# An infinity row by column points, image 0 prepared in one piece, and VectorE's operations in another order

## The chip, the cores and the metric

The kernel runs on one core of a Trainium2 chip. The metric is the device time of one execution in microseconds (us). TensorE is called PE, VectorE DVE, ScalarE ACT, GpSimd POOL and SyncE SP, as in the profile. Everything is computed in float32.

## The reference, cut

The input x has 4 images of 256 channels and 64 x 64 pixels. Each output pixel is a weighted sum of 49 neighbours of the same image, the weights coming from a softmax over a convolution; then the result is whitened over groups of 64 channels with the statistics of all images.

```python
k = conv(x, w1, padding=6, dilation=2) + b1        # 256 -> 128 channels, 7 x 7 taps
k = conv(k, w2) + b2                               # 128 -> 49, 1 x 1
attn = softmax(k, axis=1)
shifts = stack([xp[:, :, 2*u:2*u+64, 2*v:2*v+64] for u in range(7) for v in range(7)], axis=1)
y = einsum('bkchw,bkhw->bchw', shifts, attn)       # xp: x padded by 6 on each side
# whitening: mean and 64 x 64 covariance of each channel group, 5 Newton steps
# for its inverse square root, that matrix times the centred y, gain and shift
```

## The kernel before

**The convolution.** w2 is multiplied into w1, which leaves one convolution from 256 channels to 49 logits with 7 x 7 taps at distance 2. Since the distance is 2, even and odd rows and even and odd columns are separate problems. An image lies in two slots in on-chip memory, one for each row parity; the two column parities stay side by side. The 7-tap convolution is computed by evaluation and interpolation at seven points, 0, 1, -1, 2, -2, 1/2 and infinity (number 6, `INF`), first along rows and then along columns:

- `row_weights` and `weights` evaluate the weights at a row point and a column point. This is done once for each pair, at the first image that needs it. Later images load the result from DRAM (`gd`). For row points 4 and 5 the row-evaluated weights wait in DRAM (`kept`) until then.
- `row_eval` evaluates an image at one row point on VectorE and leaves it in one of three buffers `rb`.
- `col_eval` evaluates that at the column points. There is one buffer `xh` for each column point, so the next row's points can be written only when PE has read the present ones.
- `conv_bank` is PE's part: the points of a row are taken in three banks, (1, 2, 0), (3, 4, infinity) and (5). For each, matmuls of 128 columns (line L502) accumulate in one of two PSUM buffers `cv`, and ACT copies the result to `pv` (L512), which has two buffers.
- `col_interp` interpolates a row's seven column points, 22 VectorE instructions of 162 or 144 elements, and writes one plane of `zz`. One of the four output phases needs no arithmetic and is copied by ACT (L567). `row_interp` does the same over the planes, with 576 and 512 elements, and gives the logits. It has two parts: part 0 can start before the last row is there. All arithmetic of these functions goes through `add` (L300), `sub` (L303) and `madd` (L307), which therefore are VectorE's lines in the profile.

Some row points are computed without column points: `direct` convolves the rows as they are with 28 wide matmuls (L608) and needs hardly any VectorE work. Image 0 does this for row points 0, 4, 5 and infinity, and all other images for infinity alone, through `direct_inf`, which loads its weights into a buffer `wi` and leaves its result in a plane of its own, `zi`. So `rows` lists row points 1, 2, 3 for image 0, and 0 to 5 (`ROWS`) for images 1, 2, 3.

**The rest.** `softmax` transposes the logits (L797), takes the maximum (L803) and the exponentials on ACT (L811). `move_terms` and `load_band` bring the weights by way of DRAM and a VectorE transpose (L908) into a band matrix. `first_half` and `second_half` ("a half" below) make transposed blocks of x (L926, copied by ACT at L934), multiply them with the band (`weighted_sum`, L955), store y (L974), and `turn_y` (L987, L995) and `moments` (L1008) collect the covariance. At the end comes the whitening.

**The order.** PE's instructions keep the order in which they are written. Image 0 is written out by hand, and VectorE keeps the written order there too (`strict`). From image 1 on, the program is a list of `conv_step`s. Each convolves one bank, prepares the same bank of the next row, and at a row's last bank interpolates. The halves of the image before are put into gaps of this list: every step has a cost (6, 5 and 2 for the three banks, 12 for the direct infinity), and each time an eighth of the image's cost has passed, a half or a softmax follows. A scheduler orders VectorE, ACT and POOL there by priority, except at an image's end, where `in_order()` fixes VectorE's order. Before, the direct infinity stands ahead of row 0 in images 2 and 3, and after row 0 in image 1.

Of the kernel before, what the change touches and what calls it, by code (L numbers as in the profile page):

```python
# [27 lines left out]
ROWS = (0, 1, 2, 3, 4, 5)  # L28
# [3 lines left out]
def kernel(  # L32
# [222 lines left out]
    zz = apool.tile([P, NP - 1, Q9, W], F32, name="zz")  # L255
    zi = [apool.tile([P, Q9, W], F32, name=f"zi{k}") for k in range(2)]
    for k in range(2):
        nc.gpsimd.memset(zi[k], 0.0)
    ct = apool.tile([P, Q8 * 4 * Q8, 4], F32, name="ct")
    it = ct.rearrange("p a b -> p (a b)")[:, :PT].rearrange("p (q b) -> p q b", q=Q9)  # L260
# [10 lines left out]
    gd = [dram.tile([P, nsl, NSK], F32, name=f"gd{b}") for b in range(NP - 1)]  # L271
# [42 lines left out]

    def keep_weights(br):
        f = (gb5 if br == 5 else gbr).rearrange("p v a r k -> p (v a r k)")
        nc.scalar.mul(f, f, SCALE[br])
        nc.sync.dma_start(kept[br], f)

    def row_weights(br):  # L320
# [8 lines left out]
        if br == 1:  # L329
            add(E, T[6], T[4])  # L330
            add(O, T[5], T[3])
            add(S0, E, O)
            add(E1, T[2], T[0])
# [4 lines left out]
        elif br == 3:  # L338
            madd(E, T[4], 4.0, T[6])
            madd(O, T[3], 4.0, T[5])  # L340
            madd(S0, O, 2.0, E)
            madd(E1, T[0], 4.0, T[2])
            madd(S1, T[1], 2.0, E1)
        elif br == 4:
            madd(S0, O, -2.0, E)
            madd(S1, T[1], -2.0, E1)
        else:
            madd(S0, T[6], 2.0, T[5])
            madd(S0, S0, 2.0, T[4])
            madd(S0, S0, 2.0, T[3])  # L350
            madd(S1, T[2], 4.0, T[0])
            madd(S1, T[1], 2.0, S1)
            add(S1, S1, S1)

    def weights(b, br, i):
# [9 lines left out]
        wt = apool.tile([P, ns, NSK], F32, tag=f"wr{i}", name=f"wr_{b}_{br}_{i}")  # L365
# [7 lines left out]
        elif br in kept:  # L373

            f = rb[0].rearrange("p q r c w -> p (q r c w)")[:, : KS * NSK]
            if i == 0:
                nc.sync.dma_start(f, kept[br])
            f = f.rearrange("p (v a r k) -> p v a r k", v=KS, a=NCC, r=2)
            g = [f[:, v] for v in range(KS)]
        else:  # L380
            g = [gbr[:, v] for v in range(KS)]
        g = [t.rearrange("p a r k -> p (a r k)") for t in g]
        e, o, e1 = (
            ct.rearrange("p a b -> p (a b)")[:, k * NSK : (k + 1) * NSK] for k in range(3)
        )
# [4 lines left out]
        if i == 0:  # L390
            add(e, g0[0], g0[2])
            add(o, g0[1], g0[3])
            add(o0[1], e, o)
            sub(o0[2], e, o)
            add(e1, g1[0], g1[2])
# [4 lines left out]
        elif i == 1:  # L400
            madd(e, g0[2], 4.0, g0[0])
            madd(o, g0[3], 4.0, g0[1])
            madd(o0[3], o, 2.0, e)
            madd(o0[4], o, -2.0, e)
            madd(e1, g1[2], 4.0, g1[0])
# [3 lines left out]
        else:  # L409
            madd(o0[5], g0[0], 2.0, g0[1])  # L410
            madd(o0[5], o0[5], 2.0, g0[2])
            madd(o0[5], o0[5], 2.0, g0[3])
            madd(o1[5], g1[0], 4.0, g1[2])
            madd(o1[5], g1[1], 2.0, o1[5])
# [8 lines left out]
    def row_eval(b, br, rb=rb):  # L423

        for pr in range(2):
# [5 lines left out]
            elif br == 0:  # L431
                nc.scalar.copy(r[2], xs[:, 0])
            for cc in range(NCC):
                X = [xs[:, a, :, cc] for a in range(4)]
                q = [t[:, :, cc] for t in r]
                if br == 3:
                    madd(q[1], X[2], 4.0, X[0])
                    madd(q[2], X[3], 4.0, X[1])
                elif br == 5:
                    madd(q[2], X[0], 2.0, X[1])  # L440
                    madd(q[2], q[2], 2.0, X[2])
                    madd(q[2], q[2], 2.0, X[3])
# [9 lines left out]
        return rb[{1: 2, 2: 0, 3: 0, 4: 1, 5: 2, 0: 2}[br]]  # L452

    def col_eval(src, i):
# [9 lines left out]
        if i == 0:  # L464
            add(EO, X[:, :, 0:2], X[:, :, 2:4])
            add(o[1], E, O)
            sub(o[2], E, O)
            nc.scalar.copy(o[0], X4[0])
        elif i == 1:
            madd(EO, X[:, :, 2:4], 4.0, X[:, :, 0:2])  # L470
            madd(o[3], O, 2.0, E)
            madd(o[4], O, -2.0, E)
            nc.scalar.copy(o[INF], X4[3])
        else:
            madd(o[5], X4[0], 2.0, X4[1])
            madd(o[5], o[5], 2.0, X4[2])
            madd(o[5], o[5], 2.0, X4[3])

    ncv = [0]
    pvs = {}  # L480

    def conv_bank(b, br, i, w):

        if i == 0:
            pvs[b, br] = apool.tile(
                [P, NP, Q9, 2 * Q9], F32, tag="pv", name=f"pv_{b}_{br}", bufs=2
            )
# [23 lines left out]
        with tc.high_priority():  # L511
            nc.scalar.copy(  # L512
                pvs[b, br][:K2, i0 : i0 + len(pts)].rearrange("p n q b -> p (n q b)"),
                cv[:K2, : len(pts)].rearrange("p n q b two -> p (n q b two)"),
            )

    def interpolate(pt, tmp, outs, cut, part=None):

# [8 lines left out]
        if part != 1:  # L527
# [4 lines left out]
            add(s3, c0, c6)  # L532
            sub(s3, tmp, s3)
            madd(s1, tmp, -2.0, s1)
            madd(tmp, tmp, -30.5, s1)
            madd(tmp, s3, 22.5, tmp)
            madd(s1, c0, 1.5, s1)
            madd(s1, c6, -30.0, s1)
            madd(s3, s1, -1.0 / 6, s3)
            sub(s4, s4, s2)  # L540
            madd(tmp, s2, -16.0, tmp)
            add(tmp, tmp, s4)
            madd(outs[0], lo(s1), 1.0 / 6, hi(c0))
            add(outs[2], lo(c6), hi(s3))
        if part != 0:
            madd(hh, tmp, -1.0 / 9, hh)
# [5 lines left out]
    def phases(t):  # L552

        return [t[:, :, bass.ds(4 + a - R if a < R else 0, Q8, 4)] for a in range(4)]

    def col_interp(b, br, part=None):
        pv = pvs[b, br]
        pt = {c: pv[:K2, i] for i, c in enumerate(ORDER)}
        outs = phases(zz[:K2, br].rearrange("p q (w two) -> p q w two", two=2))
        cut = lambda t, k: t[:, :, 2 * k : 2 * (k + Q8)].rearrange("p q (b two) -> p q b two", two=2)  # L560
        t = it
        if part is not None:

            t = pvs[b, ROWS[-2]][:, 0]
        interpolate(pt, t[:K2], outs, cut, part)
# [818 lines left out]
```

## Time and profile before

| what | value |
|---|---|
| median of 3 runs | 761.5 us (761.24 to 763.82) |
| profiled execution | 767.08 us, span 765.3 us |
| granted PE clock | 0.978 |
| PE busy | 710.7 us (93%) |
| DVE busy | 630.3 us (82%), 1312 instructions |
| ACT busy | 332.4 us (43%) |
| POOL busy | 34.4 us (4%) |
| image 0 ends (last interpolation of rows) | 171.3 us |
| image 1 ends | 315.1 us |
| image 2 ends | 462.6 us |
| image 3 ends | 600 us |

The span runs from the first to the last instruction of the profiled execution, and that execution was 5.6 us longer than the median of the runs. A group line of the profile gives the source line, engine and operation, the tiles (out<-in), shape and count, then busy time and the mean of one instruction in ns, then the idle time of the engine ahead of them and what ended most of it. [...]

### The profile page before, as it was taken

The page shows a single profiled execution, that of the slowest core. Times are in us where ns is not written, and L with a number is a line of the kernel's source. Part 1 is how long each engine was busy: PE and PEld are TensorE (multiplying, and loading weights), DVE is VectorE, ACT ScalarE, POOL GpSimd, SP SyncE. Part 2 cuts the span into 40 slices and gives each one's busy share as a digit, 9 for nine tenths or more (in the row PEclk, how much of TensorE's full clock was granted, in tenths as well). Part 3 has the DMA queues.
Part 4 walks back from the last instruction along what each step waited for, and adds up shares of the span by engine and source line. Part 5 has one row for each costly group of instructions (what it writes and reads, how often), then busy time and mean ns, then how long its engine had stood idle before and what let it go on. Part 6 is the DMA issues. An engine that isn't in the chain of part 4 may idle for free.

```text
span 765.3 us, 18542 instructions
## 1 busy us (share of the span) xinstructions
PE 710.7 (93%) x7512; PEld 538.0 (70%) x7512; DVE 630.3 (82%) x1312; ACT 332.4 (43%) x958; POOL 34.4 (4%) x48
## 2 busy tenths in 40 slices
PE   6989899969899999989999999999999889998996
PEld 1449564365798887779988967798898768885322
DVE  3769999999899999989996899699979775645565
ACT  2413241025555454366444443635435473322464
POOL 0410000020000010001000100000000000000000
PEclk9999999979999999999999999999999999999999
DMA  8991110042654393056734920533532233362487
GB/s 323 238 322 65 39 75 38 1 155 68 200 153 156 122 351 91 20 160 205 235 120 141 313 70 1 155 90 110 166 88 80 49 115 128 115 251 111 190 362 327
DMA packets 59773, 114.76 MB, mean 150 GB/s; under 512 B 22903, under 2 KB 42024, under 8 KB 58920
## 3 DMA queue, kind: packets, MB, share of 16 engines
q1 hardware_dynamic: 55992, 94.71, 37.5%
q0 software_dynamic: 3696, 18.88, 7.2%
q8 instruction: 59, 0.97, 0.5%
q14 instruction: 26, 0.21, 0.1%
HBM read 66.23 MB, written 47.33 MB: 148 GB/s over the span
## 4 chain that ended last, share of the span: by engine, by line
DVE 43%; PE 32%; ACT 5%; issue 5%; DMA 2%; SPq 0%; DVEq 0%; ACTq 0%
PE y L955 10%; PE cv L502 7%; DVE xh L307 5%; PE tp L1324 4%; DVE rb L307 3%; DVE pv L307 3%; DVE zz L307 3%; DVE ct L307 3%; DVE ct L300 3%; DVE band L908 3%; PE sig L1008 3%; PE tp L987 2%; PE tp L926 2%; DVE pv L303 2%; DVE rb L300 2%
## 5 line engine op out<-in xcount | busy, mean ns | idle before, releaser
L502 PE MATMUL cv<-xh,wr 128*49 128x128 f32 x4368 | 253.7, 278 | 14.3 <-DVE xh L300 11.5
L502 PEld LDWEIGHTS cv<-xh,wr 128*49 128x49 f32 x4368 | 247.3, 125 | 19.9 <-issue 12.9
L955 PE MATMUL y<-band,xb 128*128 128x224 f32 (+2 forms) x640 | 153.4, 379 | 12.5 <-ACT xb L934 8.3
L955 PEld LDWEIGHTS y<-band,xb 128*128 128x128 f32 x640 | 111.2, 196 | 34.4 <-ACT xb L934 10.8
L974 ACT ACTIVATE slot<-y,pivot 128x512 f32<-128x512 f32 x53 | 36.7, 740 | 60.0 <-PE y L955 60.0
L512 ACT COPY pv<-cv 113x486 f32<-113x486 f32 (+1 forms) x63 | 29.8, 474 | 74.9 <-PE cv L502 73.7
L995 ACT COPY yt<-tp 128x256 f32<-128x256 f32 x128 | 45.5, 379 | 34.8 <-PE tp L987 33.8
L926 PE MATMUL tp<-ident,slot 128*128 128x128 f32 x256 | 50.3, 299 | 7.1 <-ACT yt L995 7.1
L987 PE MATMUL tp<-ident,slot 128*128 128x128 f32 x256 | 52.0, 299 | 4.0 <-ACT xb L934 1.4
L908 DVE STREAM_TRANSPOSE band<-band 128x960 f32<-128x960 f32 (+1 forms) x48 | 50.8, 1059 | 4.9 <-DMA band<-sd 4.8
L987 PEld LDWEIGHTS tp<-ident,slot 128*128 128x128 f32 x256 | 41.3, 205 | 13.9 <-issue 4.5
L926 PEld LDWEIGHTS tp<-ident,slot 128*128 128x128 f32 x256 | 40.0, 206 | 14.4 <-ACT yt L995 9.0
L857 ACT COPY zt<-d 32x112 f32<-32x112 f32 (+2 forms) x156 | 45.0, 288 | 1.7
L811 ACT ACTIVATE d<-tp,mx 128x49 f32<-128x49 f32 x128 | 37.0, 336 | 15.1 <-DVE mx L806 15.1
L307 DVE SCALAR_TENSOR_TENSOR xh<-ct 128x512 f32<-128x512 f32 x42 | 27.7, 681 | 12.2 <-PE cv L502 12.0
L934 ACT COPY xb<-tp 128x256 f32<-128x256 f32 x87 | 30.4, 376 | 15.8 <-PE tp L926 15.2
L1008 PE MATMUL sig<-yt 128*64 128x65 f32 x1024 | 36.9, 225 | 0.0
L1008 PEld LDWEIGHTS sig<-yt 128*64 128x64 f32 x1024 | 32.5, 138 | 6.0 <-issue 4.4
L608 PE MATMUL cv<-slot,wi 128*49 128x496 f32 (+3 forms) x168 | 34.8, 571 | 0.0
L934 DVE COPY xb<-tp 128x256 f32<-128x256 f32 x41 | 16.4, 421 | 22.2 <-PE tp L926 22.2
L307 DVE SCALAR_TENSOR_TENSOR pv<-pv 113x162 f32<-113x162 f32 x105 | 33.5, 319 | 1.0
L419 ACT ACTIVATE wr<-wr 128x392 f32<-128x392 f32 (+1 forms) x36 | 17.3, 512 | 31.1 <-DVE wr L300 18.8
(224 smaller groups left out, 999.9 us busy)
## 6 DMA issues: line engine op xcount, KB each, us to landing
out_dram<-out SPq DMA_DIRECT2D x32, 512.0 KB, 3.4
sd<-zt SPq DMA_DIRECT2D x16, 896.0 KB, 3.9
slot<-in_x_dram POOLq DMA_DIRECT2D x12, 1024.0 KB, 9.6
band<-sd SPq DMA_DIRECT2D x128, 84.0 KB, 2.1
wr<-gd SPq DMA_DIRECT2D x15, 588.0 KB, 3.8
wr<-gd SPq DMA_DIRECT2D x15, 490.0 KB, 3.6
spill<-slot POOLq DMA_DIRECT2D x3, 2048.0 KB, 8.4
back<-spill SPq DMA_DIRECT2D x3, 2048.0 KB, 7.7
```

The lines of the kernel that those rows point to most:

```text
L300: return in_turn(TT(o, a, b, ALU.add))
L307: return in_turn(STT(o, a, f, b, ALU.mult, ALU.add))
L502: nc.tensor.matmul(cv[h * HB : h * HB + KT, k, sr : sr + n, sc : sc + n], wv[:, sc, sr, cc], xh[bc][:, :n, h * NCC + cc, :n], start=(j == ...
L811: nc.scalar.activation(d[:, h, i], lt[i // NI][:, i % NI, h, :KT], AF.Exp, bias=mx[:, i, h : h + 1], accum_out=s[:, h, i : i + 1],)
L857: ins = nc.scalar.copy(o, i)
L908: nc.vector.transpose(f, f)
L926: nc.tensor.transpose(t[:, cc * P : (cc + 1) * P], xt[:, cc, CR * m : CR * (m + 1), bass.ds(pc, SW, 2)], ident,)
L934: (nc.vector.tensor_copy if tail else nc.scalar.copy)(xb, t[:, :C])
L955: nc.tensor.matmul(ps[:, cc, q0 - half * HALF : q1 - half * HALF, :], xb[:, cc * P : (cc + 1) * P], rhs, start=(k == 0), stop=(k == len(PI ...
L987: nc.tensor.transpose(t[:, cc * P : (cc + 1) * P], yt[:, cc, CR * i : CR * (i + 1), bass.ds(pc, SW, 2)], ident,)
L995: nc.scalar.copy(yb.rearrange("p a g c -> p (a g) c")[:, :, :GW], t[:, :C].rearrange("p (e c) -> p e c", c=GW),)
L1008: nc.tensor.matmul(sig[g * GW : (g + 1) * GW, cc], yb[:, cc, g, :GW], yb[:, cc, g], start=(count[0] == 0 and cc == 0), stop=(count[0] == 4 ...
```

## The change

It has four parts.

1. **Infinity in images 2 and 3.** `ROWS` begins with `INF`, so that images 2 and 3 compute this row by column points like the others: half a row of matmuls, since only one of its two taps exists. Its weights are evaluated in image 2 and kept in DRAM. `direct_inf` and its buffer are gone. Image 1 still uses `direct` for it, but the call stands at the end of image 0's part and accumulates in another PSUM buffer.
2. **Image 0.** All row points are evaluated, convolved or brought to `direct` first, and all interpolation follows. Weights and column points are interleaved (`both0`). Row 0 of image 1 is prepared partly before and partly after the last interpolation. The first softmax comes at the start of image 1.
3. **Neighbours on VectorE.** In `row_weights`, `weights`, `row_eval`, `col_eval` and `interpolate` the same operations stand in another order, so that an instruction rarely needs the result of the one just before it. For this `pv` is one tile with three slots instead of two buffers, and ACT's copy L567 of most rows is put behind the next row's second eviction (`later`). `row_interp` uses `ct` for its temporary; `zi` is gone.
4. **Costs.** The planner's costs follow, so gap 0 of images 2 and 3 now falls after the first bank of row 0 and gap 1 after the first bank of row 1.

```diff
-ROWS = (0, 1, 2, 3, 4, 5)
+ROWS = (INF, 0, 1, 2, 3, 4, 5)
...
+    NV = 3
+    pv = apool.tile([P, NV, NP, Q9, 2 * Q9], F32, name="pv")
...
+    kept[INF] = dram.tile([P, KS * NSK // 2], F32, name="gi")
+    nc.sync.dma_start(kept[INF], tap[:, UPOS[3]].rearrange("p v a k -> p (v a k)"))
...
         if i == 0:
             add(e, g0[0], g0[2])
             add(o, g0[1], g0[3])
+            add(e1, g1[0], g1[2])
             add(o0[1], e, o)
             sub(o0[2], e, o)
-            add(e1, g1[0], g1[2])
...
+            elif br == INF:
+                nc.scalar.copy(r[1], xs[:, 3])
...
+    def both0(src, br, i):
+
+        g = col_ops(src, i)
+        next(g)
+        nxt.update(weights(0, br, i, lambda: next(g)))
+        for _ in g:
+            pass
...
+        if i == 1:
+
+            while later:
+                tc.add_manual_dep(
+                    later.pop()().ins,
+                    last.ins.name,
...
             add(s3, c0, c6)
+            madd(s1, tmp, -2.0, s1)
             sub(s3, tmp, s3)
-            madd(s1, tmp, -2.0, s1)
             madd(tmp, tmp, -30.5, s1)
+            sub(s4, s4, s2)
             madd(tmp, s3, 22.5, tmp)
             madd(s1, c0, 1.5, s1)
+            madd(tmp, s2, -16.0, tmp)
             madd(s1, c6, -30.0, s1)
+            if part is None:
+                add(tmp, tmp, s4)
             madd(s3, s1, -1.0 / 6, s3)
-            sub(s4, s4, s2)
-            madd(tmp, s2, -16.0, tmp)
-            add(tmp, tmp, s4)
...
+        if b > 0:
+
+            t = pv[:K2, (at + 2) % NV, NP - 1].rearrange("p q b -> p (q b)")
...
+        if part is None and b > 0 and br != ROWS[-2]:
+            later.append(end)
+        elif part != 0:
+            end()
...
-    rows += [(b, br) for b in range(1, B) for br in ROWS]
+    rows += [(b, br) for b in range(1, B) for br in ROWS[1 if b == 1 else 0 :]]
...
-    nxt.update(weights(0, 3, 0))
-    col_eval(xr, 0)
-    direct0(0, 1)
-    nxt.update(weights(0, 3, 1))
-    col_eval(xr, 1)
-    nxt.update(weights(0, 3, 2))
+    for i in three:
+        both0(xr, 3, i)
+        if i == 0:
+            direct0(0, 1)
+    for i in three:
+        bank(2, i)
     row_weights(4)
     keep_weights(4)
     xrs[4] = row_eval(0, 4)
-    col_interp(0, 1)
-    col_eval(xr, 2)
-    bank(2, 0)
-    bank(2, 1)
     direct0(4, 0)
-    bank(2, 2)
     row_weights(5)
...
+    col_interp(0, 1)
     col_interp(0, 2)
     direct0(4, 1)
+    direct0(5, 0)
     col_interp(0, 3)
     row_interp(0, 0)
-    direct0(5, 0)
-    for i in three:
-        prepare(NR0, i)
+    prepare(NR0, 0)
     direct0(5, 1)
     row_interp(0, 1)
+
+    direct(1, INF, 0, acc[:, 0], [tap[:, UPOS[3], v] for v in range(KS)])
+    prepare(NR0, 1)
+    prepare(NR0, 2)
...
-        inf = (12, lambda b=b: direct_inf(b))
         if b == 1:
-
-            steps[:3] = [
-                *steps[:3], (0, lambda: soft(0, 0)), inf, (0, lambda: soft(0, 1)),
-            ]
-        else:
-            steps.insert(0, inf)
+            steps.insert(0, (0, lambda: soft(0, 0)))
+            steps.insert(4, (0, lambda: soft(0, 1)))
```

## The prediction

> **What bounds the kernel now.** First the engines' busy time and, beside it, the chain that ended last:
>
> ```profile
> PE 710.7 (93%) x7512; PEld 538.0 (70%) x7512; DVE 630.3 (82%) x1312; ACT 332.4 (43%) x958; POOL 34.4 (4%) x48
> ...
> DVE 43%; PE 32%; ACT 5%; issue 5%; DMA 2%; SPq 0%; DVEq 0%; ACTq 0%
> ```
>
> The reader is to see that the busier engine isn't the one that the chain names most: PE and VectorE take turns. So I read VectorE by stage (PE, PEld, DVE, ACT, POOL after the stretch and its length):
>
> ```profile
> 50.00:171.30 121.30, 106.88 (x1050) 69.68 (x1048) 116.50 (x227) 31.43 (x64) 6.73 (x8) 0.95 0.21 77
> 171.30:315.70 144.40, 138.21 (x1634) 112.41 (x1631) 139.26 (x306) 72.50 (x229) 5.78 (x5) 0.99 0.48 154
> 315.70:463.20 147.50, 141.81 (x1840) 124.04 (x1840) 131.13 (x268) 72.78 (x226) 8.03 (x7) 0.99 0.51 162
> 463.20:601.00 137.80, 132.01 (x1764) 120.18 (x1761) 123.75 (x258) 67.92 (x220) 0.15 (x1) 0.99 0.33 98
> ```
>
> These are image 0 and the convolutions of images 1, 2 and 3. VectorE has 4.8 and 5.1 us to spare in the first two, and 16.4 and 14.1 us in the last two. Images 0 and 1 are its own; in 2 and 3 it and PE wait for each other. After 601 us comes the tail, which the change doesn't touch.
>
> What neighbours cost shows in VectorE's timeline (start, duration):
>
> ```profile
> 303.29 0.32 DVE L303 TENSOR_TENSOR pv<-pv 113x162 f32<-113x162 f32 x1
> 303.64 0.33 DVE L300 TENSOR_TENSOR pv<-pv 113x162 f32<-113x162 f32 x1
> 304.00 0.33 DVE L303 TENSOR_TENSOR pv<-pv,pv 113x162 f32<-113x162 f32 x1
> ...
> 337.06 0.32 DVE L307 SCALAR_TENSOR_TENSOR pv<-ct,pv 113x162 f32<-113x162 f32 x1
> 337.30 0.32 DVE L300 TENSOR_TENSOR pv<-pv 113x162 f32<-113x162 f32 x1
> 337.54 0.32 DVE L303 TENSOR_TENSOR pv<-pv 113x162 f32<-113x162 f32 x1
> ```
>
> Same shape, same duration, but starts 0.36 us apart where each needs its predecessor, 0.24 where none does: **0.12 us for a dependent neighbour**. One instruction between is enough. The same difference stands at 512 elements (0.60 against 0.72) and 576 (0.67 against 0.79). So I cost VectorE by starts, not by durations.
>
> Last, PE's timeline at the change to image 2 and the waits of ACT:
>
> ```profile
> 300.81 11.59 PE L608 MATMUL cv<-slot,wi 128*49 128x512 f32 x56
> ...
> 320.19 1.12 PE L797 MATMUL tp<-ident,lgx 113*128 113x113 f32 x8
> 321.24 10.03 PE L502 MATMUL cv<-xh,wr 128*49 128x128 f32 x176
> ...
> 335.25 0.52 PE L926 MATMUL tp<-ident,slot 128*128 128x128 f32 x2 [1.88 <-ACT yt L995]
> ```
> ```profile
> ACT zz L567 <- DVE pv L307: 50.4, 17, 7.1
> ```
>
> L608, the direct infinity row, fills PE while VectorE ends image 1. The half after the first softmax is slow (331.20 to 342.57, 11.4 us, where others take 7.7) because exponentials and copies fill ACT. And 17 times ACT stands in the copy L567 until VectorE has ended an interpolation.
>
> [...]
>
> **The change, part by part.**
>
> *VectorE's order.* In the two built programs' lists, instructions that wait for their immediate predecessor fall from 276 to 118: 158 x 0.12 = **19.0 us** less. By stage: image 0 130 to 48 (-9.8), image 1 30 to 6 (-2.9), image 2 45 to 21 (-2.9), image 3 58 to 30 (-3.4); the tail is as before.
>
> *The infinity row of images 2, 3.* PE: 28 wide matmuls (11.6 us) become 52 of 128 columns, half a row; a row of 208 records took 11.76 us, so 5.9. Saved 5.7 us twice. VectorE gains per image 9 instructions of column points (two of 1024 at 1.14, seven of 512 at 0.60: 6.5 us) and 22 of interpolation (5.2 us), and once 20 of weights (98 columns, 0.17: 3.4 us). That is +15.1 in image 2, +11.7 in image 3. With the order: -9.8, -2.9, **+12.2, +8.3**, in all +7.8 us. ACT gains two copies of 128x1024 (1.05 each) and three evictions (0.5 each) per image, and loses one; it is 43% busy. SP's queue loses the `wi` loads and gains one load of kept weights, three stores and three loads of gd (wr<-gd lands in 3.8 us), issued a row ahead; the load writes rb[0], free by then. Cover gone, each would cost its 4 us once. POOL's memsets after gpool.release wait for the moved L608; it ends earlier than before.
>
> *Image 0 first; image 1's infinity ahead.* VectorE bound from 50 us, so image 0 ends at about 171.3 - 9.8 = 161.5. L608 of image 1 (11.6 us) goes into PE's gaps there and is no longer ahead of row 0.
>
> *Image 1* is VectorE's: row_interp ended at 315.1, now 315.1 - 9.8 - 2.9 = 302.4.
>
> *Change to image 2.* After that VectorE must still do 9.1 us (summed from the list: rest of the infinity row, and of row 0 its first column points) until row 0's bank 0 can start: 311.5. It ends 5.4 us later (316.9); the half, which the planner now puts behind it since the infinity row counts 6.5 and not 12, and the softmax transposes (7.6 + 1.1) end at 325.6. Before, the same work was done at 321.24 + 5.4 = 326.6. **Of 12.7 us, 1 is left**: PE had L608 and the half done while it waited, now it waits with nothing to do. Then row 0's other banks (6.4) to 332; row 1's bank 0 needs points that the list puts at 302.4 + 31.0 = 333.4; it ends at 338.8, the next half and softmax at some 348 if ACT is freer there (+0.5), against 343.62 + 7.2 = 350.8. So **-3**.
>
> *Change to image 3.* Counted from 420.60, where PE starts row 4's last banks. Before: row 0's bank 0 ended at 473.60 + 5.4, 58.4 later, half and softmax within. Now VectorE needs 12.2 us to the start of row_interp (433.47 before, less 0.7 by the order) and 33.3 (list) to row 0's first points: 45.5. PE needs only 11.8 + 5.5 + 6.4 + 9.3 + 5.9 = 38.9, so it idles 6.6. Then 5.4 + 7.6 + 1.1: 59.6. **+1 to +4, taken +3**, as transposes of the band come between.
>
> *Softmax of image 2* (483.56 to 494.71, 11.2): its half now comes a bank later, away from the exponentials: 3.5 less, of which I take **-2**. *L567 deferred, third pv slot:* PE waited 15.2 us for ACT's xb and yt copies between 150 and 603; a fifth of it: **-3**. Alone on a busy VectorE it would be 0, at best -8.
>
> Sum: -3 + 3 - 2 - 3 = -5. The profiled execution took 767.08 us (span 765.3), 5.6 above the median; it becomes 762, and the median 761.5 becomes **756**.
>
> **Rivals.**
> 1. *The early gain is kept whole.* PE's waiting at the image changes is filled (VectorE catches up in its 16.4 us of slack). Then -12.7 stays, +3 falls away, with part of ACT: 748, at best 744. For it: the slack. Against: the lists put row 0's points behind the infinity row. Chance 0.2.
> 2. *PE's chain decides.* From 202 us PE's records follow each other; the 11.4 us saved turn into idle time, and ACT brings nothing: 761. That VectorE's order does not matter[...] ends here or worse. Chance 0.15.
> 3. *Slower.* VectorE's slack in images 2, 3 is waiting at image changes for PE to free the single xh buffers (xh L307 waited 12 us for L502), and can't be filled. Then +12.2 + 8.3 comes in full against -12.7: +8, 769. It decides once less than about 8 of the 30 us of slack is used. For it: the infinity row falls where VectorE has no pause. Against: in the middle of both images PE is the later one. Chance 0.2.
>
> **How the numbers follow.** The forecast has 0.45 (751 to 760). Half a per cent (3.8 us) is about what a measurement here can tell: faster is under 757.7, slower above 765.3. Forecast: 0.38 faster, 0.07 same; rival 1 all faster; rival 2 same; rival 3 slower. Faster 0.58, same 0.22, slower 0.20. The range 744 to 768 reaches from the best of rival 1 to just short of rival 3's own value, and leaves out the upper part of rival 3 alone.
>
> **What would show it.** Right: VectorE x1394; interpolation starts 0.24 apart; image 0 ends near 161, image 1 near 302; PE idle 5 to 8 us before row 0 of image 3, named by DVE xh. Wrong: image 0 not 8 us earlier (the order), or image 2's middle 10 us earlier (rival 1), or row 0 of image 3 later than 474 (rival 3).

## The result and the profile after

The change makes the kernel slower by half a per cent. The median of 20 runs is 765.44 us (761.8 to 776.25), that of the kernel before 761.52 us (756.27 to 764.05, 20 runs). The ratio is 1.0059, 95% interval 1.004 to 1.0078. A second set of runs gave 1.0046 (1.0025 to 1.0068). The prediction had 756 us, a gain.

The page after, engines and chain, as they were shown of before:

```profile
PE 698.6 (92%) x7608; PEld 539.3 (71%) x7608; DVE 643.0 (85%) x1394; ACT 342.8 (45%) x980; POOL 33.7 (4%) x45
...
DVE 44%; PE 41%; ACT 5%; DMA 4%; issue 4%; SPq 1%; DVEq 0%; ACTq 0%
```

PE has 12 us less to do, VectorE 13 us more, and the counts are the forecast ones (7608 and 1394). By stage, in the same stretches as before:

```profile
50.00:171.30 121.30, 119.29 (x1194) 71.32 (x1190) 114.99 (x237) 39.66 (x107) 6.66 (x7) 1.00 0.21 75
171.30:315.70 144.40, 123.12 (x1618) 113.06 (x1619) 139.56 (x328) 70.03 (x200) 5.64 (x4) 0.94 0.49 152
315.70:463.20 147.50, 136.07 (x1819) 124.06 (x1820) 135.23 (x288) 77.33 (x236) 8.03 (x7) 0.98 0.52 165
463.20:601.00 137.80, 132.99 (x1764) 121.97 (x1761) 129.11 (x284) 68.58 (x222) 1.00 (x6) 0.98 0.34 102
```

In the stretch of image 1 PE now stands idle for 21 us. The edges are those of the first trace of before, and the changed kernel's images end elsewhere. Cut at each kernel's own image ends, images 2 and 3 read as follows, first before (its second trace, r4_before, see below), then after:

```profile
309.30:455.60 146.30, 140.37 (x1839) 123.24 (x1839) 131.09 (x267) 72.63 (x226) 8.03 (x7) 1.00 0.51 163
455.60:592.20 136.60, 130.72 (x1767) 119.58 (x1764) 124.20 (x259) 67.97 (x220) 0.15 (x1) 1.00 0.32 99
...
299.40:457.00 157.60, 145.59 (x1962) 132.82 (x1958) 145.14 (x312) 81.32 (x245) 8.03 (x7) 0.99 0.53 165
457.00:596.60 139.60, 131.46 (x1765) 121.30 (x1766) 133.21 (x290) 68.13 (x221) 0.15 (x1) 0.97 0.33 99
```

VectorE has 14.1 and 9.0 us more to do, and the two images took 11.3 and 3.0 us longer. Of the 27.6 us that it had to spare, only 8.8 were taken up: 2.8 in image 2 and 6.0 in image 3.

The new order does what it was meant to do. VectorE's timeline, in the last interpolation of image 1's columns:

```profile
287.54 0.32 DVE L303 TENSOR_TENSOR pv<-pv 113x162 f32<-113x162 f32 x1
287.77 0.32 DVE L310 SCALAR_TENSOR_TENSOR pv<-pv 113x162 f32<-113x162 f32 x1
288.01 0.32 DVE L306 TENSOR_TENSOR pv<-pv 113x162 f32<-113x162 f32 x1
```

Neighbours start 0.24 us apart where before they started 0.36 apart. What it is worth is lost at the image changes. PE's timeline, images 1 to 2 and 2 to 3:

```profile
297.06 2.87 PE L531 MATMUL cv<-xh,wr 128*49 128x128 f32 x48
303.48 4.12 PE L531 MATMUL cv<-xh,wr 128*49 128x128 f32 x40 [3.55 <-DVE xh L310]
308.31 6.42 PE L531 MATMUL cv<-xh,wr 128*49 128x128 f32 x112 [0.71 <-ACT pv L541]
...
322.27 1.17 PE L846 MATMUL tp<-ident,lgx 113*128 113x113 f32 x8
```
```profile
450.66 2.67 PE L531 MATMUL cv<-xh,wr 128*49 128x128 f32 x40 [0.56 <-DVE xh L310]
460.68 8.08 PE L531 MATMUL cv<-xh,wr 128*49 128x128 f32 x112 [7.34 <-issue]
...
476.28 1.12 PE L846 MATMUL tp<-ident,lgx 113*128 113x113 f32 x8
```

The reader is to see the idle times in brackets: between the infinity row's banks PE has nothing to do. "issue" at 460.68 says that the profile shows no releaser, but VectorE's timeline does:

```profile
456.34 0.69 DVE L310 SCALAR_TENSOR_TENSOR lgx<-zz 113x512 f32<-113x512 f32 x1
456.95 0.69 DVE L310 SCALAR_TENSOR_TENSOR xh<-rb 128x512 f32<-128x512 f32 x1
457.55 1.22 DVE L303 TENSOR_TENSOR ct<-rb 128x1024 f32<-128x1024 f32 x1
458.69 0.69 DVE L310 SCALAR_TENSOR_TENSOR xh<-xh,rb 128x512 f32<-128x512 f32 x1
459.29 0.68 DVE L303 TENSOR_TENSOR xh<-ct 128x512 f32<-128x512 f32 x1
459.89 0.68 DVE L310 SCALAR_TENSOR_TENSOR xh<-xh,rb 128x512 f32<-128x512 f32 x1
```

Column point 5 of the infinity row takes three dependent operations. The first comes right after the last operation of image 2's row interpolation, each of the others behind one of row 0's, and the third ends at 460.57, 0.1 us before PE goes on.

Behind this gap of 7.34 us PE is slow as well. The same stretch by windows; the third number from the end is the granted clock:

```profile
453.40:457.40 4.00, 0.00 (x0) 0.00 (x0) 3.90 (x6) 2.05 (x4) 0.00 (x0) 0.99 0.44 125
457.40:464.20 6.80, 3.52 (x34) 3.55 (x36) 6.80 (x12) 0.68 (x2) 0.00 (x0) 0.50 0.07 15
464.20:476.00 11.80, 11.80 (x150) 10.77 (x147) 11.77 (x28) 4.07 (x10) 0.00 (x0) 1.00 0.20 62
```

For the first 3.3 of these 6.8 us PE was still idle, which costs nothing more. The rest slowed the 112 records of matmuls at 460.68: they took 8.08 us, where 112 took 6.42 at full clock (at 308.31). From there PE works without a pause to the softmax at 476.28, so these 1.7 us are lost. At the change to image 2 the half clock (303.8 to 307.2) lay on the 40 records at 303.48, and there it cost nothing, for VectorE had column point 5 of the infinity row ready only at 308.16:

```profile
307.48 0.68 DVE L310 SCALAR_TENSOR_TENSOR xh<-xh,rb 128x512 f32<-128x512 f32 x1
```

**Which trace of before to compare with.** The first one (767.08 us) is longer than every one of the other 20 executions. The waits of VectorE in it, from 30 to 60 us, hold a wait for image 0's input:

```profile
DVE rb L300 <- DMA slot<-in_x_dram: 6.5, 1, 6.5
```

A second trace of the same kernel (r4_before, 756.32 us, span 754.5) has no such wait, and its stages lie 6 to 9 us earlier. It is near the shortest execution of before (755.98), as the changed kernel's trace (761.8) is its shortest, so these two are compared. The changed kernel's other trace (r0_after) lies 1.9 to 3.6 us later at the marks of the table, so a difference of 1 to 2 us between neighbouring marks says little. Marks are the softmaxes' first transposes on PE. With the change a first softmax has row 0's first bank ahead of it (5.4 us), a second has 7.2 us more ahead of it (row 0's third bank, row 1's first); both are taken off.

| mark | before, second trace | changed | difference, like for like | forecast |
|---|---|---|---|---|
| image 1, first softmax | 313.7 | 322.3 | +3.2 | -1 |
| image 1, second | 334.9 | 343.1 | +1.0 | -3 |
| image 2, first | 464.9 | 476.3 | +6.0 | 0 |
| image 2, second | 485.4 | 496.7 | +4.1 | -2 |
| image 3, first | 597.8 | 603.6 | +5.8 | -5 |
| span | 754.5 | 760.0 | +5.5 | -5 |

### The profile page after: what moved, and what is told of

Its sections match the earlier page's. It is cut to its first block, busy times and chain, and to the rows that moved or that the text cites. A ratio compares the mean times of both kernels' runs of the same rounds, so it can differ in the third digit from the quotient of the medians.

```text
span 760.0 us, 18845 instructions
## 1 busy us (share of the span) xinstructions
PE 698.6 (92%) x7608; PEld 539.3 (71%) x7608; DVE 643.0 (85%) x1394; ACT 342.8 (45%) x980; POOL 33.7 (4%) x45
## 4 chain that ended last, share of the span: by engine, by line
DVE 44%; PE 41%; ACT 5%; DMA 4%; issue 4%; SPq 1%; DVEq 0%; ACTq 0%
PE cv L531 9%; PE y L1004 8%; PE acc L668 6%; DVE xh L310 6%; DVE pv L310 5%; DVE rb L310 4%; PE tp L1370 4%; DVE ct L310 3%; DVE band L957 3%; DVE ct L303 3%; DVE zz L310 3%; DVE pv L306 2%; PE tp L1036 2%; PE tp L975 2%; PE sig L1057 2%
## 5 line engine op out<-in xcount | busy, mean ns | idle before, releaser
L531 PE MATMUL cv<-xh,wr 128*49 128x128 f32 (+1 forms) x4576 | 268.8, 279 | 19.5 <-issue 7.3
L531 PEld LDWEIGHTS cv<-xh,wr 128*49 128x49 f32 x4576 | 260.6, 126 | 25.5 <-issue 18.0
L1004 PE MATMUL y<-band,xb 128*128 128x224 f32 (+2 forms) x640 | 151.2, 374 | 15.0 <-ACT xb L983 12.9
L1004 PEld LDWEIGHTS y<-band,xb 128*128 128x128 f32 x640 | 109.6, 193 | 36.4 <-ACT xb L983 16.0
L541 ACT COPY pv<-cv 113x486 f32<-113x486 f32 (+1 forms) x69 | 33.2, 483 | 101.8 <-PE cv L531 101.5
L310 DVE SCALAR_TENSOR_TENSOR pv<-pv 113x162 f32<-113x162 f32 x215 | 63.8, 318 | 0.5
L310 DVE SCALAR_TENSOR_TENSOR xh<-ct 128x512 f32<-128x512 f32 x46 | 30.3, 683 | 10.2 <-PE cv L531 10.2
L983 ACT COPY xb<-tp 128x256 f32<-128x256 f32 x87 | 30.4, 376 | 12.7 <-PE tp L975 12.0
L306 DVE TENSOR_TENSOR pv<-pv 113x162 f32<-113x162 f32 x112 | 34.6, 319 | 0.4
L668 PE MATMUL acc<-slot,tap 128*49 128x496 f32 (+3 forms) x168 | 34.6, 569 | 0.0
```

The lines of the kernel that those rows point to most:

```text
L306: return in_turn(TT(o, a, b, ALU.subtract))
L310: return in_turn(STT(o, a, f, b, ALU.mult, ALU.add))
L531: nc.tensor.matmul(cv[h * HB : h * HB + KT, k, sr : sr + n, sc : sc + n], wv[:, sc, sr, cc], xh[bc][:, :n, h * NCC + cc, :n], start=(j == ...
L668: nc.tensor.matmul(ps[h * HB : h * HB + KT, :, w0:w1_], w[v][:, cc], xs[:, :, cc, w0 + d : w1_ + d], start=(j == 0), stop=(j == len(order) ...
L983: (nc.vector.tensor_copy if tail else nc.scalar.copy)(xb, t[:, :C])
L1004: nc.tensor.matmul(ps[:, cc, q0 - half * HALF : q1 - half * HALF, :], xb[:, cc * P : (cc + 1) * P], rhs, start=(k == 0), stop=(k == len(PI ...
```

## The experiments

All ratios are to the kernel before on the same chip, with 95% intervals. Two theories stood at the start: the waits of PE (W), or the granted clock (C).

**r0_after: the changed kernel again.**

> The changed kernel again, for a second trace of it beside others on one chip. Two theories of why it is 4 us slower than before although its one trace is 5 us shorter. Theory W (waits): the infinity row's VectorE work at the two image changes leaves TensorE idle for 7 + 4 us and takes back what the order and image 0 gave; then this trace again shows gaps of about 3.5 and 7 us ahead of row 0 of images 2 and 3, and the time is 763 to 767. Theory C (clock): the stages are shorter, but the granted TensorE clock is lower in most executions than in that trace (0.970 to 0.976 against 0.978), each 0.001 being some 0.8 us; then the time of single executions follows their clock, and the execution at the highest clock takes about 762.

Measured: 764.55 us, ratio 1.0046. The gaps are there again (4.2 us at 275, 3.3 at 302, 7.4 at 456). Times follow the clock: the 45 executions of before that were measured beside it have a correlation of -0.92 between time and clock, with 0.49 us for 0.001. But before has a median clock of 0.980 and the changed kernel one of 0.975, and a line through each kernel's executions (29 of the changed one, from both sets) gives 761.5 and 761.9 us at 0.980. So most of the difference shows as clock. The traces say where the lower clock comes from: between 50 and 650 us PE runs at half clock for 6.8 us in r4_before (clock 0.991), for 23.9 us in the first trace of before (0.978) and for 27.3 us in both traces of the changed kernel (0.978 and 0.975); in r4_before and the changed kernel each piece stands behind an idle time of 1.6 us or more. In all 18 traces every idle time of PE over 2.4 us in that stretch was followed by half clock within 5 us of its start. In the changed kernel's first trace these were 5.4 us of idle time from 184.5 (half clock from 187.7), 4.3 from 273.3 (276.4), 3.6 from 299.9 (303.8) and 7.3 from 453.3 (457.4). So in these traces half clock follows the gaps, and what theory C saw is, as far as they show, a part of W's price.

**r4_before: the kernel before, a second trace.** Nothing is edited.

> The kernel before, once more, for a second trace. In its first trace (767.08 us) VectorE waited 6.5 us for image 0's input at 46.91; in the traces of the changed kernel and of the two part versions there is no such wait. If that wait was an accident of the one execution, this trace has none, its stages lie about 6 us earlier, and it takes 756 to 763 us; then all gains that the prediction counted against the first trace hold, but 6 us of what the two traces differ by is no gain. If it belongs to the kernel's order, it is here again, and the time is near 767.

Measured: 756.32 us, no wait for the input. The wait was an accident of the first execution.

**r1_order: the new order alone.**

The kernel before, with the changed kernel's `row_weights` and `interpolate`, and the same exchanges in `weights` and `row_eval`, such as:

```diff
-            add(o0[1], e, o)
-            sub(o0[2], e, o)
             add(e1, g1[0], g1[2])
+            add(o0[1], e, o)
+            sub(o0[2], e, o)
```

> The kernel before, with the new order of VectorE's operations in row_weights, weights, row_eval and interpolate alone: dependent neighbours fall from 276 to 172, 12.5 us of VectorE's time. By theory W it keeps a good part, since it adds no row: 752 to 757. By theory C the clock falls[...], and it gains little: 758 to 762 with a clock below that of the kernel before. If VectorE's order doesn't matter at all: 761.5.

Measured: 755.03 us, ratio 0.9938 (0.9917 to 0.9959). The order is a gain by itself, and the clock did not fall with it but rose (median 0.988). Its first softmax of image 1 comes at 311.6, 2.0 us ahead of r4_before, and the later marks 3 us ahead. That is about half of the 6.5 us; the rest goes with the clock: at 0.988 the line through the executions of before gives 757.6.

**r2_direct: the change with the direct infinity row in images 2 and 3.**

```diff
-ROWS = (INF, 0, 1, 2, 3, 4, 5)
+ROWS = (0, 1, 2, 3, 4, 5)
...
+        else:
+            steps.insert(0, (12, lambda b=b: direct_inf(b)))
```

> The changed kernel with the infinity row of images 2 and 3 computed directly as before, ahead of row 0 and at a cost of 12 in the plan (its weights are loaded into rb[1]); image 0, the order, pv's slots and the later copy are those of the change. Theory W: TensorE has its 11.6 us of work at the image changes again, VectorE 26.8 us less: 5 to 8 us faster than the changed kernel, 756 to 760. Theory C: within 3 us of the changed kernel, at a clock as low.

Measured: 757.27 us, ratio 0.9961 (0.9937 to 0.9984). The column-point rows cost 0.85 to 1 per cent, some 7 us; without them the change gains in the median. Its shortest execution (755.67) is hardly shorter than that of before (755.98). From the first softmax of image 1 to that of image 2 this version takes 147.4 us, the changed one 154.0.

**r7_old0: r2_direct with image 0 in the old order.**

Image 0's part is that of the kernel before, and behind it stands image 1's direct infinity (against the kernel before):

```diff
     row_interp(0, 1)
+    direct(1, INF, 0, acc[:, 0], [tap[:, UPOS[3], v] for v in range(KS)])
```

> The version with the direct infinity in images 2 and 3 (757.3 us), with image 0 written out in the order of the kernel before, image 1's direct infinity still at the end of that part. The order alone gave 755.0. If image 0's new order costs those 2 us (it leaves two parts of row 0's preparation to image 1, where VectorE has no time to spare): 754 to 756. If pv's third slot and the later copy cost them: 757 to 759.

Measured: 758.51 us, 0.9968 (0.9952 to 0.9984), the same as r2_direct. Image 0's order neither brings nor costs anything that can be told. What separates both from the order alone (some 2 us, with intervals that overlap) is then among pv's slots, the later copy, the other temporary, image 1's infinity ahead and the place of image 0's softmaxes; it was not taken apart further. It shows as clock: a median of 0.979 and 0.980 here, against 0.988 with the order alone, which at 0.49 us for 0.001 is worth 4 us.

**r3_gap: the half ahead of row 0's first bank.**

```diff
-                        (cost * len(taps(br)) / 2, lambda k=k, i=i: conv_step(k, i))
+                        (cost, lambda k=k, i=i: conv_step(k, i))
```

> The changed kernel with the infinity row's banks counted as 6, 5 and 2 in the plan instead of half: the first half of images 2 and 3 then comes ahead of row 0's first bank, and the second after its second bank, as before the change. Theory W: TensorE does a half (8 us) while VectorE prepares row 0, so the gaps there nearly go: 4 to 8 us faster than the changed kernel, less up to 3 us if the second half falls among the exponentials again. Theory C: the gaps go, but the time follows the clock: within 3 us of the changed kernel.

Measured: 764.52 us, 1.0042 (1.0029 to 1.0056), as the changed kernel. The gaps stayed, 3.4 and 7.4 us, because they lie between the infinity row's own banks, ahead of where the half was put. So this edit didn't put the theories to the test.

**r5_fill: the half right behind the infinity row's first bank.**

```diff
-        for cost, f in steps:
+        for n, (cost, f) in enumerate(steps):
...
-            if at * NPC >= (j + 1) * whole:
+            if n == 0 if b > 1 and j == 0 else at * NPC >= (j + 1) * whole:
```

> The changed kernel with the first half of images 2 and 3 put right behind the infinity row's first bank, where TensorE stood idle for 3.6 and 7.3 us and then ran at half clock for 3.4 and 6.8 us. Theory W (TensorE's waiting is the loss): both gaps are filled and no clock is lost there: 752 to 758. Theory D (VectorE is the bound at the image changes, and TensorE's idle time only shows it): row 0 of image 3 starts no earlier than before this edit, gaps appear behind the half instead, 762 to 766.

Measured: 767.77 us, 1.0088 (1.0055 to 1.012). Both gaps are filled, and the wait stands one row later and is longer:

```profile
334.00 8.27 PE L531 MATMUL cv<-xh,wr 128*49 128x128 f32 x96 [8.35 <-DVE xh L303]
```

This is row 1's first bank in image 2. Theory W falls. D stands in kind, though the time lies above its range: around this wait VectorE is the later one (busy 24.77 of 25 us from 325 to 350), and filling PE's gaps moved its idle time and did not remove it.

**r6_mid: the infinity row between rows 2 and 3.**

```diff
-ROWS = (INF, 0, 1, 2, 3, 4, 5)
+ROWS = (0, 1, 2, INF, 3, 4, 5)
```

> The changed kernel with the infinity row between rows 2 and 3 of images 2 and 3 instead of ahead of row 0: its VectorE work (11.7 us an image) then falls into the middle, where TensorE is the later one, and the image changes have neither it nor a direct convolution. Theory W: TensorE has 5.9 us less to do at the changes, but row 0 is ready 9 us earlier: 755 to 760. Theory D: VectorE is relieved where it is the bound: 752 to 757. If the place doesn't matter and only the sum of VectorE's work does: 763 to 766.

Measured: 762.5 us, 1.0012 (0.9997 to 1.0027). Some 2 us better than ahead of row 0, less than W and D said, and next to what was written for the case that the place doesn't matter: new gaps of 5.0 us at 373 and 3.5 at 518 came up in the middle. So the image change is not the only place where the row costs.

**r8_xh5, r9_xh5d: the last bank prepared ahead of row_interp,** in the changed kernel and in r2_direct.

```diff
                     col_interp(b, br, 1)
+                    if k + 1 < len(rows):
+                        prepare(k + 1, i)
                     row_interp(b, 1)
...
                 col_interp(b, br)
                 if last:
+                    prepare(k + 1, i)
                     row_interp(b, 0)
```

> The changed kernel with the last bank of the next row prepared (the three operations of column point 5, and its weights) between col_interp and row_interp at an image's end, in the fixed order; in the changed kernel two of the three slip in between row_interp's operations and the last comes behind it, and TensorE waits 4.3 us in image 1 (trace at 273 to 287) and 7.3 us ahead of row 0 of image 3. Theory S (the new order starves this chain: row_interp's operations, now independent, always go first): both waits fall to under 2 us and the half clock behind them goes; 757 to 761. Theory D (VectorE is simply the bound there, and the wait moves to the next row, as when the half was moved): 763 to 767.

> The same edit on the version with the direct infinity in images 2 and 3 (757.3 us), where TensorE waits 5.6 us at 281 for column point 5 of image 1's last row and runs at half clock for 6.8 us after it. There VectorE has 26.8 us less to do, so both theories differ less: by S 751 to 755; if the wait moves on, 756 to 758.

Measured: r8 768.69 us, 1.0099 (1.0072 to 1.0127); r9 756.27 us, 0.9933 (0.9909 to 0.9957). In r2_direct PE waited in image 1 for the same three operations, which the scheduler had put between those of row_interp:

```profile
286.98 0.88 PE L531 MATMUL cv<-xh,wr 128*49 128x128 f32 x6 [5.60 <-DVE xh L310]
```

In r9 that wait is gone (a shorter one, 2.8 us for a copy of ACT, stands at 284), and the first softmax of image 1 comes at 313.3 instead of 317.5. Its time is 1 us better, within the intervals, and in the range written for a wait that moves on. In r8 the wait moved: 9.1 us at 299, for the infinity row's points, and the time lies above both ranges. So where the row is direct theory S holds for the wait and not for the time; where it is not, D holds.

**r10_noint: without the infinity row's interpolation.**

```diff
+        if br == INF:
+            for a, c in ((0, 0), (2, 1), (1, 2)):
+                add(outs[a], cut(pt[c], 0), cut(pt[5], 1))
+        else:
...
```

> The changed kernel with 19 of the 22 operations of the infinity row's column interpolation left out in images 2 and 3 (its planes get other values; everything else is computed as before): 4.5 us of VectorE an image less, nothing on TensorE, and no transfer. TensorE never waits for this interpolation directly. By theory D time falls by nearly what VectorE saves, 9 us less what it waits elsewhere: 756 to 760. If TensorE's waits come from the order of single operations and not from VectorE's sum: 762 to 765.

Measured: 762.69 us, 1.002 (1.0006 to 1.0035). Nine us of VectorE bring 2. The 7.4 us gap is untouched. VectorE's sum alone is not what decides.

**r11_rb1: the infinity row's weights by way of rb[1].** In the changed kernel's image 1, ACT's and PE's timelines show:

```profile
276.85 0.27 ACT L405 COPY wr<-rb 128x98 f32<-128x98 f32 x1 [5.10 <-DMA rb<-gi]
277.03 0.27 ACT L406 COPY wr<-rb 128x98 f32<-128x98 f32 x1
277.20 0.36 ACT L983 COPY xb<-tp 128x256 f32<-128x256 f32 x1
```
```profile
277.62 1.17 PE L1004 MATMUL y<-band,xb 128*128 128x96 f32 x4 [4.32 <-ACT xb L983]
```

The load into rb[0] waits for row 5's weights there, ACT waits for the load, xb's copy waits behind it, and PE for xb.

```diff
-            f = rb[0].rearrange("p q r c w -> p (q r c w)")[:, : KS * nk]
+            f = rb[1 if br == INF else 0].rearrange("p q r c w -> p (q r c w)")[:, : KS * nk]
...
-                nc.scalar.copy(r[1], xs[:, 3])
+                nc.scalar.copy(r[0], xs[:, 3])
```

> The changed kernel with the infinity row's kept weights loaded into rb[1] and its image rows copied to rb[0], instead of the other way round. In the changed kernel the load into rb[0] has to wait for row 5's weights there; ACT's copy of the infinity row's weights stands 5.1 us for it (trace at 276.85), the copy of xb queued behind it comes late, and TensorE idles 4.3 us in a half and then runs at half clock for 6.8 us. Theory Q (this queue is a part of the loss): the idle time at 273 goes, image 1 ends 4 to 7 us earlier on TensorE, 758 to 762. If VectorE is the only bound there: 763 to 766.

Measured: 763.85 us, 1.0033 (1.0017 to 1.005). ACT's wait is gone, but PE then waits 4.8 us at 281 for column point 5 and the first softmax of image 1 is no earlier (322.7). The jam is real and hidden behind VectorE.

**r12_warm, r13_warmd: extra work in the gaps,** in the changed kernel and in r9_xh5d.

```diff
+    def warm(n):
+        t = tp()
+        for _ in range(n):
+            pe(nc.tensor.transpose(t[:, :P], ident, ident))
...
         conv_bank(b, br, i, w)
+        if br == INF and i == b - 2:
+            warm(11 if b == 2 else 22)
```

In r13 the condition is `(b, br, i) == (1, 1, 2)`, with `warm(16)`.

> The changed kernel with TensorE kept busy in the two gaps of the infinity rows by extra transposes of the identity whose result nobody reads: 11 (3.2 us) behind the first bank in image 2, 22 (6.4 us) behind the second in image 3. They take no time off any wait. Theory H (each idle stretch of TensorE is followed by half clock, which is part of the price): no half clock after the two gaps, 3.4 x 0.5 + 6.8 x 0.5 = 5 us of TensorE's time back, 759 to 763. If the clock falls for another reason, or the stretch behind the gaps isn't what decides: 764 to 767.

> The version with the direct infinity and the last bank prepared ahead of row_interp (756.3 us), with 16 such transposes (4.6 us) where TensorE idles 5.6 us at 184, ahead of row 2 of image 1, and then runs at half clock for 6.8 us. Theory H: 3 us of TensorE's time come back; if TensorE is the later one up to the end of image 1, 753 to 755; if VectorE is, as the prediction had it for image 1, 756 to 757.

Measured: r12 765.42 us, 1.005 (1.0033 to 1.0067); r13 754.77 us, 0.9901 (0.988 to 0.9921). A transpose of the identity took 0.12 us and not the 0.29 that the expectation used (16 in r13 took 1.97), so the gaps were filled by a third only. In r12 idle times of 2.3 and 4.8 us stayed, and so did half clock behind them. PE's timeline in images 2 and 3:

```profile
308.16 8.06 PE L531 MATMUL cv<-xh,wr 128*49 128x128 f32 x112 [2.34 <-DVE xh L310]
...
462.74 7.70 PE L531 MATMUL cv<-xh,wr 128*49 128x128 f32 x112 [4.80 <-issue]
```

The same two stretches took 6.42 and 8.08 us in the changed kernel. So in image 2 the edit pushed the half clock onto work that had run at full clock, 1.6 us worse, and in image 3 it saved 0.4. The median clock rose from 0.975 to 0.978, but what left was half clock under idle time, and the time stayed. This run says nothing against theory H. In r13 the half clock behind the gap at 184 fell from 6.8 to 3.4 us (the 96 records of matmuls behind it took 7.04 us, in r9 8.15) and the first softmax of image 1 came 1.6 us earlier; against r9 the time is 1.5 us shorter, with intervals that just overlap. Of the versions that compute what the reference asks for, r13 has the shortest median, with r1_order next to it.

**r14_nopts, r15_none: without the infinity row's column points, and without its interpolation too.**

```diff
         nxt.update(w)
+        if br == INF:
...
+                nc.scalar.copy(o, X[:, :, a].rearrange("p (e b) two -> p e b two", b=Q8))
+            return
         col_eval(cur["x"], i)
```

> The changed kernel with the nine VectorE operations of the infinity row's column points left out in images 2 and 3, 6.5 us an image (its matmuls read what the row before left in xh; ACT's copies, the weights, all matmuls and the interpolation stay). Theory P (what costs is the points' place in VectorE's chain from the last interpolation of one image to row 0 of the next, where TensorE has nothing else to do): the 7.3 us gap and most of the 3.6 us gap go, 8 to 11 us faster than the changed kernel: 754 to 758. Theory V (VectorE's sum over the image, wherever it falls): 13 us less should bring half as much again as leaving out the interpolation did (2 us for 9): 761 to 763. If neither the points nor the gaps matter: 764.

> The same with 19 of the 22 operations of the infinity row's column interpolation left out as well: of the row's VectorE work only its weights (3.4 us in image 2) stay, TensorE has 11.4 us less than with the direct row. Theory P: within 2 us of the run with the points left out, since the interpolation lies beside other work: 753 to 758. Theory V: 3 to 5 us below that run.

Measured: r14 756.72 us, 0.9947 (0.9924 to 0.9969); r15 753.33 us, 0.9895 (0.9875 to 0.9915). PE's timeline in r14, images 2 to 3:

```profile
445.07 6.04 PE L531 MATMUL cv<-xh,wr 128*49 128x128 f32 x104
452.93 5.53 PE L531 MATMUL cv<-xh,wr 128*49 128x128 f32 x96 [1.82 <-DVE xh L303]
...
466.00 1.18 PE L852 MATMUL tp<-ident,lgx 113*128 113x113 f32 x8
```

The infinity row is one stretch of 6.04 us, and the softmax comes 10 us earlier than in the changed kernel. In image 2 less was gained: a gap of 3.9 us stayed at 301, now for the load of row 0's weights (`wr<-gd`), and its first softmax is 3 us earlier. 13 us of VectorE taken from the points bring 8 us, 9 us taken from the interpolation bring 2 (r10) or 3 (r15 against r14). So what costs is the points, for which PE waits, and little the interpolation, for which it doesn't. That their place at the image change is the reason, as theory P has it, isn't shown: in the middle of the image the row cost nearly as much (r6). Theory P also had r15 within 2 us of r14; that was too narrow.

## Why the prediction was wrong, point by point

The forecast summed to -5 us; the traces compared give +5.5. The 10.5 us between them are, in the order of the sum: 2.8 by the end of image 1, 1.4 at the change to image 2, 2.0 at the change to image 3 and 4.4 in the last term, at most 0.2 in the softmaxes. The mechanism, that PE would wait for VectorE at the image changes, was forecast and came; what failed is sizes, each time on the hopeful side.

- **VectorE's order: right in kind, short by 3 us in images 0 and 1.** Counts and the 0.12 us hold, and so do the 0.17 us that were taken for 98 columns (starts at 286.12 and 286.29). The forecast moved the end of image 1's interpolation by -12.7 us; it ended at 299.3 instead of 309.2 in r4_before, -9.9. (Image 0's own end, 150.8, says nothing: two of the three parts of row 0's preparation now stand behind it.) What is missing is covered by new waits in image 0, which the list of VectorE alone couldn't show: 4.7 us between 40 and 152, where r4_before has 0.6. The longest (at 83) is 3.6 us for a result of PE's direct row, which VectorE now reaches before PE:

```profile
DVE zz L303 <- ACT zz L682: 3.9, 2, 3.6
```

- **The change to image 2: the mechanism right, the size short.** The forecast counts from the start of row_interp's last operation (315.1, 302.4), which is 298.7 here. From there to the end of the softmax's transposes it had 23.2 us; it took 24.7 (to 323.4). VectorE needed 10.0 us and not 9.1 to row 0's first points, and the infinity row's third bank (0.9 us) still stood ahead of row 0 on PE. With the 2.8 us above, the "-1" became +3.2. That PE would have nothing to do was right.
- **The change to image 3: the wait right, its price short.** Forecast +3, measured +5.0 (from +1.0 to +6.0). The idle time itself was near (6.6 forecast, 7.3 found), though it stands ahead of the infinity row's third bank and not of row 0. Not priced was what follows it: half clock on the matmuls behind the gap (0.50 from 457.4 to 464.2), 1.7 us (8.08 against 6.42), about what is missing. The forecast could have read it in the first trace of before: behind an idle time of 5.6 us from 151.95 the granted clock is 0.50 there from 154.7 to 161.5, and 96 records took 7.43 us, where 96 took 5.53 in r14 (at 452.93):

```profile
157.53 7.43 PE L502 MATMUL cv<-xh,wr 128*49 128x128 f32 x96 [5.58 <-DVE xh L300]
```

- **Infinity's weights load: wrong.** "The load writes rb[0], free by then" is wrong, row 5's weights are there. It cost ACT 5.1 us and PE 4.3, but r11 shows that nothing else was gained by removing it.
- **Softmaxes: right.** -2 was forecast for each; the marks moved by -2.2 and -1.9.
- **L567 and the third slot, -3: the largest miss, nothing came.** It was a fifth of PE's 15.2 us of waits for ACT's xb and yt copies between 150 and 603, taken without a chain that leads from those waits to the end. ACT's wait for the interpolation did fall from 50.4 to 31.8 us. PE's waits became 17.6, 4.3 of them from the weights load above; leaving those out, they fell by 2. From the second softmax of image 2 to the end the changed kernel took 1.4 us more than r4_before, like for like, and 0.1 less than the first trace of before: no gain shows. The slots and the later copy were not run alone.

```profile
ACT zz L622 <- DVE pv L310: 31.8, 9, 5.7
...
PE y L1004 <- ACT xb L983: 12.9, 14, 4.3
```

- **The rivals.** The third was nearest: the infinity row falls where VectorE has no pause, and the slack in images 2 and 3 takes up only part of it. It was to decide below about 8 us of used slack; 8.8 were used, and the time lies between forecast and rival. Its reason, that the xh buffers hold the slack, was not tested. The order's worth (r1) excludes the reading that dependent neighbours cost nothing.
- **The traced execution.** The forecast took the first trace's 5.6 us over the median for an offset without effect. It was a wait for the input, which took no part in the sums, but it made the changed trace (761.8, 5.3 us shorter) look like the forecast 762. That agreement was chance: an unlucky execution of before beside the luckiest of the changed kernel.

The parts, by ratio: order alone -0.6%; with slots, later copy and image 1's infinity ahead -0.3%; with image 0's order -0.4%; with the infinity rows +0.5%. Open stays which part of the second step takes half of the order's gain back; it goes with a clock that is lower by 0.008.

## What to carry to other kernels

Saving the busier engine's work with the help of another one doesn't pay where that other engine is the later one at that very place (here two rows with 5.7 us less of PE's work each made the kernel some 7 us longer than r2): count the operations that must lie between two hand-overs, not the sum over a stage. Where a program changes from one stage to the next, a stretch of independent work for the waiting engine is worth more than it seems (the direct row's 11.6 us here), and moving work into a gap moves the gap when the other engine is the bound (r5: 8.35 us, one row later). A wait of PE costs more than its idle time if half clock falls on the work behind it (1.7 us behind the 7.3 us here). An order in which neighbours don't depend was a gain (0.6% in r1), but it also lets a block of high priority run without a pause, and what used to slip in between comes late (column point 5 here: PE waited 5.6 us for it in r2).

## What the runs showed of the hardware

- VectorE started an instruction 0.12 us later if it waited for its immediate predecessor (0.36 against 0.24 us at 162 elements); with one instruction between them it cost nothing (338.49, 338.74 and 338.97 in the first trace of before, the third needing the first). 104 such waits fewer made the kernel 0.6% faster (r1).
- Single executions of one kernel differ by up to 1% with the granted clock (755.98 to 763.72 us, 0.49 us for each 0.001, in the 45 executions of before beside r0_after). Half clock came in pieces of 3.4 us (303.8 in the changed kernel's trace), 6.8 (457.4) or 10.2 (r5, behind 8.35 us of idle time: clock 0.80 from 325 to 350). In the 18 traces, from 50 to 650 us, every idle time of PE over 2.4 us was followed by one within 5 us of its start, and idle times of 1.6 to 2.4 us in part: in the first trace of before 2.36 us at 200.3 were, 2.08 at 51.7 were not. One piece there, at 489.2, has only 1.13 and 0.62 us of idle time ahead of it. Half clock cost time only where PE had work: 112 records of matmuls with some 3.4 us of it on them took 8.06 (r12, at 308.16) and 8.08 us (the changed kernel, at 460.68) instead of 6.42.
- 16 transposes of the identity took 1.97 us, 0.12 each (r13); 4 records of block transposes of x start within 0.58 us, 0.145 each (287.74 to 288.32 in the changed kernel's trace).
